# A graph-transformer kernel on one core: the usual arm's instructions in written order, with norm, linears and table pieces placed by step counters

## The chip, the core and the metric

The kernel runs on one core of a Trainium2 chip. The core has TensorE (PE: matmuls into PSUM, PEld: its weight loads), VectorE (DVE), ScalarE (ACT), GpSimd (POOL, which here issues the indirect DMAs) and SyncE (SP, which issues plain DMAs). Each engine takes its own instructions in the order of its queue. The metric is the device time of one execution in microseconds (us): 3934.97 us as the median of 10 runs of the kernel before (3932.45 to 3940.0).

## What is computed

Two layers of a heterogeneous graph transformer on 6250 nodes with 128 features (8 heads of 16), 100000 edges sorted by destination, 16 node types and 32 edge types; then a linear layer, a residual and a layer norm. Cut to what matters:

```
k, q, v = typed_linear(x, ntype, Wk), (.. Wq), (.. Wv)      # one 128x128 matrix per node type
kT, vT  = einsum(k, Watt), einsum(v, Wmsg)                  # for every node and every edge type
a       = sum_d(kT[src, etype] * q[dst]) * pri[etype] / 4   # one number per edge and head
att     = softmax of a over the edges of a destination
hag     = sum over the edges of a destination of att * vT[src, etype]
h       = silu(typed_linear(hag, ntype, Wa))
h       = h * alpha + x * (1 - alpha)                       # alpha = sigmoid(skip[ntype])
h       = (h - mean) * rsqrt(var + 1e-5) * g + b
# after two such layers: out = layernorm(x + h @ ff_w + ff_b)
```

All is float32.

## The kernel before

**Tables.** For each layer there is a table in DRAM with one row of 256 floats (kT and vT) for every pair of node and edge type: 200704 rows of 1 KB. Layer 0's is made first, together with a ranking of the nodes (the preparation, lines 239 to 674). Layer 1's table is made while layer 0's edges are worked on, from layer 0's result.

**Blocks and superblocks.** The ranking sorts nodes into 4 classes of 4 node types each, and within a class by falling degree, into 13 blocks of 128 nodes (52 in all). A block has as many *slots* as its deepest node may have edges; by `slots_of_blocks` (line 40) these are 40, 23, 21, 19, 18, 17, 17, 16, 15, 14, 13, 12, 11 in each class, 944 in a layer. One slot of a block is one indirect gather: 128 table rows, one per destination node, 128 KB. Three or four blocks make a superblock (line 188); a class has four, with 3, 3, 3 and 4 blocks and so 84, 54, 48 and 50 slots. There are 16.

**Edges** (`edges`, line 735), per block. ScalarE copies the queries of the block into PSUM (`qw`, line 744). For each chunk of up to 4 slots GpSimd issues the gathers into a `kv` tile (line 754; 12 such tiles), VectorE multiplies by the query (766) and reduces per head (768). After the last chunk VectorE adds the mask, takes the maximum and subtracts it (773 to 778), ScalarE takes Exp (780), VectorE sums the weights (782), multiplies the v half by the weight (790), adds up the chunks (795) and reduces (796). `normalized` (802) divides by the sum when the superblock is done.

**Nodes** (`nodes`, line 841), per superblock, a Python generator that yields between its steps: transpose `hag` (a TensorE matmul with the identity, line 215), mask it for each of the class's 4 types (`xm`, VectorE, line 200) and multiply by Wa (line 209), tanh (856), transpose back, mix with the old rows, statistics and norm (865 to 874), transpose. In layer 0 then the three linears for the next layer's k, v and q (`wkqv`, 209), q to DRAM, and the table pieces. In layer 1 then the final linear, residual, norm, and an indirect scatter of each block's output (922).

**Table pieces** (`table_block`, line 218), per block two pieces (16 edge types each), each in two halves (k, v). A half is 4 matmuls with 32 rows (line 229; the trace holds two records for each matmul) and 4 copies of 128x512 from PSUM to the tile `st` by ScalarE (line 236). After two halves `store` scatters the 2 MB tile into layer 1's table by an indirect DMA on GpSimd's queue (line 891). There are 104 such scatters. `st` has 3 buffers; a buffer is free again when its scatter has landed. All gathers of layer 1 wait for all of these scatters.

**Queries**: in layer 0 (`queries0`, line 719) transposes, masks, matmuls with Wq, a copy and a transpose back; in layer 1 (`queries1`, 729) a load.

**The order of the work.** `beside` (line 1006) chains the queries of the next superblock and the nodes of the one before it, pieces included; `edges` takes one step of it after each chunk and one after Exp, and runs off what is left when its blocks are done. After the last superblock its nodes run alone. This is only the order in which the program is written: the framework's scheduler, from priorities and its model of costs, then decides the order of instructions in each engine's queue, and may move them.

PSUM has 8 banks of 128x512 floats: `qwp` 2, `accp` 2 and `nps` 4, the last for all transposes, linears and table halves (the tile name `nb`).

## Time and profile before

| | us |
|---|---|
| median of 10 runs | 3934.97 |
| the profiled execution | 3931.96 |
| its span | 3930.0 |
| busy PE, DVE, ACT, POOL in the span | 1971.1, 2143.6, 921.6, 2056.4 |
| first gather of layer 0 starts | 916.4 |
| first gather of layer 1 starts | 2587.1 |
| last gather starts | 3869.4 |
| a scatter of a table piece from issue to landing, median in layer 0 | 10.8 |
| a gather from issue to landing, median | 2.8 |

A busy share here is an average over very different stages, so the span is read by its stages. A line of waits names the waiting instruction, what released it, the total, the number of times and the longest. A gap of 0.3 us between two of GpSimd's DMA issues stands there even when it waits for nothing. The granted clock of TensorE is either 0.5 or 1.0 at any moment in these records; a share in between is an average over time.

### The profile page before, as it was taken

How to read it: one execution, taken by the hardware profiler on the slowest of the kernel's cores; microseconds unless marked ns; L12 is line 12 of the kernel's file. 1: busy time of each engine (PE TensorE's matmuls, PEld its weight loads, DVE VectorE, ACT ScalarE, POOL GpSimd, SP SyncE). 2: the span in 40 equal slices, each digit the busy share in tenths (PEclk: the TensorE clock that was granted, in tenths of full speed). 3: DMA queues.
4: the chain of work that ended last, by engine and by line, in shares of the span. 5: the costliest groups of instructions: out<-in, count | busy, mean ns of one | idle time of the engine just before them, and what ended most of it. 6: DMA issues, size and time to landing. Idle time of an engine off the chain costs nothing. (4 is left out here: it accounts for less than half of the span.)

```text
span 3930.0 us, 25934 instructions
## 1 busy us (share of the span) xinstructions
PE 1971.1 (50%) x6850; PEld 1041.0 (26%) x6850; DVE 2143.6 (55%) x4929; ACT 921.6 (23%) x1928; POOL 2056.4 (52%) x2157
## 2 busy tenths in 40 slices
PE   2899957993166555666466657820221221121122
PEld 1345523331033333333234334410110110011011
DVE  6975632432655555455545554126655665665565
ACT  0244313451033232333233324420000000000000
POOL 0000072004766667656665664057776776777773
PEclk9999977995565566666666666755555555555555
DMA  4467548787366554675466558543343343333331
GB/s 89 160 273 310 235 130 328 322 342 243 105 216 218 204 205 164 245 263 207 145 239 257 200 176 305 204 159 115 110 113 95 116 113 101 110 111 106 105 103 51
DMA packets 216823, 716.14 MB, mean 182 GB/s; under 512 B 64437, under 2 KB 122670, under 8 KB 191615
## 3 DMA queue, kind: packets, MB, share of 16 engines
q0 software_dynamic: 110592, 459.50, 35.5%
q1 hardware_dynamic: 83425, 245.01, 16.3%
q10 hardware_dynamic: 22642, 9.82, 1.1%
q8 instruction: 58, 0.95, 0.1%
q14 instruction: 106, 0.87, 0.1%
HBM read 289.27 MB, written 438.40 MB: 185 GB/s over the span
## 5 line engine op out<-in xcount | busy, mean ns | idle before, releaser
L754 POOL DMA_INDIRECT kv<-tab,ell x1888 | 1794.0, 950 | 928.8 <-issue 506.2
L236 ACT COPY st<-nb 128x512 f32<-128x512 f32 x1420 | 737.8, 597 | 662.5 <-PE nb L229 425.9
L766 DVE TENSOR_TENSOR kv<-kv,qw 128x512 f32<-128x512 f32 (+3 forms) x512 | 326.1, 640 | 921.7 <-DMA kv<-tab,ell 886.2
L229 PE MATMUL nb<-bdv,kvT 32*128 32x512 f32 x832 | 388.2, 1050 | 143.0 <-ACT st L236 142.4
L229 PE MATMUL nb<-bdk,kvT 32*128 32x512 f32 x832 | 366.5, 1017 | 118.7 <-ACT st L236 118.7
L644 PE MATMUL l<-xm,wkqv 128*128 128x512 f32 (+1 forms) x832 | 394.9, 607 | 7.9 <-DVE xm L200 7.9
L215 PE MATMUL nb<-ident,hag 128*128 128x128 f32 x104 | 24.5, 366 | 596.9 <-DVE hag L809 596.9
L768 DVE TENSOR_REDUCE a<-kv 128x32 f32<-128x512 f32 (+3 forms) x512 | 319.8, 634 | 0.9
L566 POOL DMA_INDIRECT ell<-kvs,start x52 | 54.8, 1053 | 502.2 <-DVE gap L545 486.6
L200 DVE SCALAR_TENSOR_TENSOR xm<-ntb,nb 128x384 f32<-128x384 int32 (+1 forms) x256 | 133.1, 580 | 311.4 <-PE nb L215 311.4
L215 PE MATMUL nb<-ident,hs 128*128 128x128 f32 x104 | 32.6, 457 | 520.2 <-DVE hs L874 482.1
L891 POOL DMA_INDIRECT tab<-st,row x104 | 104.5, 1005 | 337.0 <-ACT st L236 322.3
L780 ACT ACTIVATE qw<-a 128x136 f32<-128x136 f32 (+11 forms) x104 | 30.7, 296 | 997.9 <-DVE a L778 980.1
L229 PEld LDWEIGHTS nb<-bdv,kvT 32*128 32x128 f32 x832 | 190.0, 285 | 263.1 <-ACT st L236 262.3
L795 DVE TENSOR_TENSOR acc<-kv,acc 128x512 f32<-128x512 f32 (+3 forms) x408 | 257.8, 632 | 0.2
L234 DVE COPY st<-nb 128x512 f32<-128x512 f32 x196 | 134.8, 688 | 212.2 <-PE nb L229 109.8
L790 DVE TENSOR_TENSOR kv<-kv,qw 128x512 f32<-128x512 f32 (+3 forms) x408 | 246.5, 623 | 0.0
L229 PEld LDWEIGHTS nb<-bdk,kvT 32*128 32x128 f32 x832 | 174.8, 276 | 213.2 <-ACT st L236 204.0
L644 PEld LDWEIGHTS l<-xm,wkqv 128*128 128x128 f32 x832 | 149.3, 195 | 237.1 <-issue 206.8
L229 PE MATMUL nb<-bdv,yT 32*128 32x512 f32 x784 | 169.3, 686 | 69.1 <-ACT st L236 66.3
L200 DVE SCALAR_TENSOR_TENSOR xm<-ntb,hT 128x512 f32<-128x512 int32 (+1 forms) x208 | 133.7, 656 | 113.6 <-PE l L644 104.0
L209 PE MATMUL nb<-xm,wkqv 128*128 128x384 f32 (+1 forms) x384 | 177.3, 630 | 20.0 <-DVE xm L200 20.0
(197 smaller groups left out, 2330.3 us busy)
## 6 DMA issues: line engine op xcount, KB each, us to landing
tab<-st SPq DMA_DIRECT2D x98, 2048.0 KB, 7.5
kv<-tab,ell POOLq DMA_INDIRECT x1888, 2.8
ntb<-typed SPq DMA_DIRECT2D x24, 192.0 KB, 3.2
xrd<-xr SPq DMA_DIRECT2D x13, 256.0 KB, 2.3
hr<-in_x_dram SPq DMA_DIRECT2D x10, 256.0 KB, 3.3
ntb<-in_node_type_dram SPq DMA_DIRECT2D x10, 256.0 KB, 6.9
hr<-xrd SPq DMA_DIRECT2D x12, 192.0 KB, 2.7
hrd<-hs SPq DMA_DIRECT2D x12, 192.0 KB, 2.4
```

Source lines behind the costliest of these rows:

```text
L200: nc.vector.scalar_tensor_tensor(xm[:, :n], ntb[:, :n], float(t), hT[:, :n], op0=ALU.is_equal, op1=ALU.mult)
L209: nc.tensor.matmul(ps[:, :n], w[:, t, :], xm[:, :n], start=(t == types[0]), stop=(t == types[-1]))
L229: nc.tensor.matmul(pt, yT[s, i * P:(i + 1) * P], bd[s, tt, :], start=True, stop=True)
L234: nc.vector.tensor_copy(to, pt)
L236: nc.scalar.copy(to, pt)
L644: nc.tensor.matmul(ps[i][:, :n], wkqv[:, i, t, :], xm[:, :n], start=(t == 0), stop=(t == TY - 1))
L754: get = nc.gpsimd.indirect_dma_start(out=kv[:, j - j0, :], out_offset=None, in_=tabs[l][:], in_offset=bass.IndirectOffsetOnAxis(ap=ell[:, ...
L766: nc.vector.tensor_tensor(kk, kk, qw[:, :D].unsqueeze(1).to_broadcast([P, j1 - j0, D]), op=ALU.mult)
L768: nc.vector.tensor_reduce(a[:, j0:j1, :], kk.rearrange("p k (h d) -> p k h d", h=H), axis=AX.X, op=ALU.add)
L790: nc.vector.tensor_tensor(to.rearrange("p k (h d) -> p k h d", h=H), v.rearrange("p k (h d) -> p k h d", h=H), w[:, j0:j1, :].unsqueeze(3) ...
L795: nc.vector.tensor_tensor(acc[:, :c], v, acc[:, :c], op=ALU.add)
L891: put = nc.gpsimd.indirect_dma_start(out=tabs[1].rearrange("(n t) c -> n (t c)", t=16), out_offset=bass.IndirectOffsetOnAxis(ap=row2[:, tg ...
```

## The change

The arm that is taken when the graph fits the slots (`arm(True)`) runs under `manual_schedule`: each engine's queue holds the instructions in the order in which the program is written. The program then places the work itself:

- `spread` gives a generator a rate in steps per slot; `tick`, called twice per chunk, advances the first entry of the list `work` and then the first of the list `pieces`. `work` holds the queries of the next superblock and the nodes of the one before. `pieces` holds the table pieces of the superblock before that. `rush` runs a generator off at once.
- The pieces leave `nodes` and become `pieces_of`. Each yield of `table_block` counts as two steps, and a scatter is issued three steps after its tile was handed over, so behind the matmuls and copies of two more halves. The output's scatters come six steps after their data, except in the last superblock. In the last superblock of layer 0, VectorE makes 2 of each 4 copies of a half.
- The second half of a block's edge work (`weighed`: sums, weights, chunks) is placed beside the next block's chunks, and the query of the next block is copied right after Exp.
- The superblocks of a class have 4, 3, 3, 3 blocks and so 103, 52, 45, 36 slots.
- PSUM: `qwp` 2, `accp` 1, `nps` 2 for transposes and linears, and 3 banks (`tps`, tile `tb`) for the table halves.
- The three linears k, v, q run one after the other over kept masks, a step each. The old rows `hr` are loaded in `nodes` (in layer 0 a second time, beside the load for the queries), `xr` one step earlier. The scaling of layer 1's edge weights moves into the first superblock's nodes.

The core of the diff:

```diff
--- before.py
+++ after.py
...
+    def scale_edge_weights():
+
         nc.vector.tensor_scalar(prit, prit, 1.0 / float(HS) ** 0.5, None, op0=ALU.mult)
         nc.vector.tensor_tensor(bdk, bdk, prit.unsqueeze(2).to_broadcast([P, RT, 2 * HS]),
                                 op=ALU.mult)
...
     load_edge_weights(0)
+    scale_edge_weights()
...
-                    pt = ps_pool.tile([P, SB * P], F32, name="nb").rearrange(
+                    pt = ps_pool.tile([P, SB * P], F32, name="tb").rearrange(
...
-        qwp = ctx2.enter_context(tc.tile_pool(name="qwp", bufs=2, space=PSUM))
-        accp = ctx2.enter_context(tc.tile_pool(name="accp", bufs=2, space=PSUM))
-        nps = ctx2.enter_context(tc.tile_pool(name="nps", bufs=4, space=PSUM))
+
+        if fast:
+            qwp = ctx2.enter_context(tc.tile_pool(name="qwp", bufs=2, space=PSUM))
+            accp = ctx2.enter_context(tc.tile_pool(name="accp", bufs=1, space=PSUM))
+        nps = ctx2.enter_context(tc.tile_pool(name="nps", bufs=2 if fast else 5, space=PSUM))
+        tps = ctx2.enter_context(tc.tile_pool(name="tps", bufs=3, space=PSUM))
...
-                    sbs.append((c * CB + i0, k, range(c * TC, (c + 1) * TC)))
+                    sbs.append((c * CB + CB - i0 - k, k, range(c * TC, (c + 1) * TC)))
+            sbs.sort(key=lambda sb: sb[0])
...
-            hr = npl.tile([P, SB, D], F32, name="hr", bufs=3)
+            hr = npl.tile([P, SB, D], F32, name="hr", bufs=2)
...
+        def q_rows(ps, k, tag):
+
+            qT = npl.tile([P, SB * P], F32, name="qT", tag="th")
...
+            q = ep.tile([P, SB, D], F32, name="q", tag=tag, bufs=2 if tag == "q" else 1)
...
-            got.append((q, types_of(i0, k), old_rows(hrd, i0, k)))
-            yield
...
-        def edges(l, i0, k, q, beside):
...
+        def edges(l):
...
+            queries = queries1 if l else queries0
+            got, work, pieces = [], [], []
+            for _ in queries(got, *sbs[0]):
+                pass
+
+            def spread(work, gen, steps, slots):
+
+                work.append([gen, steps / slots, 0.0])
+
+            def tick(n):
+                for of in (work, pieces):
+                    if of:
+                        w = of[0]
+                        w[2] += w[1] * n
+                        while w[2] >= 1.0:
+                            w[2] -= 1.0
+                            if next(w[0], of) is of:
+                                of.pop(0)
+                                break
+
+            def rush(of, gen):
+                while any(w[0] is gen for w in of):
+                    for _ in of.pop(0)[0]:
+                        pass
+
+            def slots(s):
+                return sum(KB[b] for b in range(sbs[s][0], sbs[s][0] + sbs[s][1]))
+
+            def query(s, i):
                 qw = qwp.tile([P, 512], F32, name="qw")
-                nc.scalar.copy(qw[:, :D], q[:, i, :])
...
-                    kk = kv[:, :j1 - j0, :D]
-                    nc.vector.tensor_tensor(
-                        kk, kk, qw[:, :D].unsqueeze(1).to_broadcast([P, j1 - j0, D]), op=ALU.mult)
-                    nc.vector.tensor_reduce(a[:, j0:j1, :],
-                                            kk.rearrange("p k (h d) -> p k h d", h=H),
-                                            axis=AX.X, op=ALU.add)
-                    next(beside, None)
-                av = a[:, :K, :]
-                nc.vector.tensor_tensor(
-                    av, av, neg[:, KO[b]:KO[b] + K].unsqueeze(2).to_broadcast([P, K, H]),
...
-                nc.scalar.activation(w, av, AF.Exp)
-                next(beside, None)
+                nc.scalar.copy(qw[:, :D], got[s][0][:, i, :])
+                return qw
+
+            def weighed(s, i, chunks, kvt, w, sums, den):
+
                 nc.vector.tensor_reduce(den[:, i, :], w.rearrange("p k h -> p h k"),
                                         axis=AX.X, op=ALU.add)
-
                 acc = accp.tile([P, CH, D], F32, name="acc")
                 for (j0, j1), kv in zip(chunks, kvt):
...
+                    yield
                 nc.vector.tensor_reduce(sums[:, i, :], acc.rearrange("p k c -> p c k"),
                                         axis=AX.X, op=ALU.add)
-            for _ in beside:
+                i0, k, _ = sbs[s]
+                if i == k - 1:
+                    hag = normalized(sums, den, i0, k)
+                    spread(work, nodes(l, *sbs[s], hag, got[s][1], lambda gen: table(s, gen)),
+                           16, pace(s + 1))
+
+            def pace(s):
+                s = min(s, len(sbs) - 1)
+                return slots(s) - 0.5 * KB[sbs[s][0]]
+
+            tables = {}
+
+            def table(s, gen):
+
+
+                if gen is None:
+                    if s - 2 in tables:
+                        rush(pieces, tables[s - 2])
+                else:
+                    tables[s] = gen
+                    spread(pieces, gen, 8 * sbs[s][1] + 4, (1.0 if s + 4 < len(sbs) else 0.6) * slots(min(s + 2, len(sbs) - 1)))
+
+            sums_of = None
+            qw = query(0, 0)
+            for s, (i0, k, types) in enumerate(sbs):
+                asked = None
+                if s + 1 < len(sbs):
+                    asked = queries(got, *sbs[s + 1])
+                    spread(work, asked, 6, 0.5 * KB[i0])
+                sums = ep.tile([P, SB, D], F32, name="sums")
+                den = ep.tile([P, SB, H], F32, name="den")
+                for i in range(k):
+                    b = i0 + i
+                    K = KB[b]
+                    a = ep.tile([P, max(KB), H], F32, name="a")
+                    w = qw[:, D:D + K * H].rearrange("p (k h) -> p k h", h=H)
...
+                        kk = kv[:, :j1 - j0, :D]
...
+                        tick((j1 - j0) / 2)
+                        if sums_of:
+                            next(sums_of, None)
+                        tick((j1 - j0) / 2)
+                    if sums_of:
+                        for _ in sums_of:
+                            pass
+                    av = a[:, :K, :]
...
+                    nc.scalar.activation(w, av, AF.Exp)
+                    sums_of = weighed(s, i, chunks, kvt, w, sums, den)
+
+                    if i + 1 < k:
+                        qw = query(s, i + 1)
+                    elif asked:
+                        rush(work, asked)
+                        qw = query(s + 1, 0)
+            for _ in sums_of:
                 pass
-            return normalized(sums, den, i0, k)
+            while work or pieces:
+                for of in (work, pieces, pieces, pieces):
+                    if of and next(of[0][0], of) is of:
+                        of.pop(0)
...
-        def nodes(l, i0, k, types, hag, ntb, hr):
+        def nodes(l, i0, k, types, hag, ntb, table):
             n = k * P
             last = l == L - 1
+            final = fast and i0 + k == NB
+            hr = old_rows(hrd if last else xrd, i0, k)
+            hT = transposed(nps, lambda i: hag[:, i, :], k)
+            yield
+            y = nps.tile([P, SB * P], F32, name="nb")
+            typed_linear(npl, types, ntb, hT, n, [(y, wa)])
+            yield
+
+            th = npl.tile([P, SB * P], F32, name="th")
+            nc.scalar.activation(th[:, :n], y[:, :n], AF.Tanh, scale=0.5)
 
             hb = npl.tile([P, SB, D], F32, name="hb")
             for i in range(k):
                 nc.scalar.activation(hb[:, i, :], hr[:, i, :], AF.Copy,
                                      scale=beta[:, l, i0 + i:i0 + i + 1])
-            hT = transposed(nps, lambda i: hag[:, i, :], k)
...
+            if last:
+                xr = npl.tile([P, SB, D], F32, name="xr", tag="hr", bufs=2)
+                nc.sync.dma_start(xr[:, :k], rows(xrd, i0, k))
+            else:
+                nc.sync.dma_start(rows(hrd, i0, k), hs[:, :k])
             yield
             if not last:
-                nc.sync.dma_start(rows(hrd, i0, k), hs[:, :k])
-                ps = [nps.tile([P, SB * P], F32, name="nb") for _ in range(3)]
-                typed_linear(npl, types, ntb, hT, n, [(ps[i], wkqv[:, i]) for i in range(3)])
+                if fast and i0 == 0:
+                    scale_edge_weights()
+                if fast:
+
+                    xms = list(masked(npl, types, ntb, hT, n))
+                    yield
+                    table(None)
+                outs = []
+                for j in range(3):
+                    ps = nps.tile([P, SB * P], F32, name="nb")
+                    outs.append(ps)
+                    if fast:
+                        for t, xm in xms:
+                            nc.tensor.matmul(ps[:, :n], wkqv[:, j, t, :], xm[:, :n],
+                                             start=(t == types[0]), stop=(t == types[-1]))
+                        yield
+                        if j < 2:
+                            to = npl.tile([P, SB * P], F32, name=f"kvT{j}", bufs=2)
+                            nc.scalar.copy(to[:, :n], ps[:, :n])
+                            outs[j] = to
...
+                q = yield from q_rows(outs[2], k, "qn")
                 yield
...
                 nc.sync.dma_start(rows(qrd[1], i0, k), q[:, :k])
...
-                    yield from table_block(ep, nps, kT, vT, i, (), 3 if fast else 2, store)
+                table(pieces_of(i0, k, outs[0], outs[1], (1, 3) if final else ()))
...
-            xr = npl.tile([P, SB, D], F32, name="xr", tag="hb")
-            nc.sync.dma_start(xr[:, :k], rows(xrd, i0, k))
...
-                stats(mv, i, f[:, s])
...
+            yield
+            for i in range(k):
+                stats(mv, i, f[:, i * P:(i + 1) * P])
...
-                nc.gpsimd.indirect_dma_start(
-                    out=out, out_offset=bass.IndirectOffsetOnAxis(ap=node[:, b:b + 1], axis=0),
-                    in_=o[:, i, :], in_offset=None, bounds_check=N - 1, oob_is_err=False)
+                if final:
+                    put_out(o, i0, i)
+
+            for _ in range(6):
+                yield
+            for i in range(0 if final else k):
+                put_out(o, i0, i)
+
+        def pieces_of(i0, k, kT, vT, share):
+
+
...
+            def scatter(tg, st, b):
...
+            def steps(gen):
+
+                for _ in gen:
+                    for _ in range(2):
+                        for what in late:
+                            what[0] -= 1
+                        while late and late[0][0] <= 0:
+                            scatter(*late.pop(0)[1])
+                        yield
+
+            for i in range(k):
+                def store(tg, st, b=i0 + i):
+                    late.append([3, (tg, st, b)])
+
+                yield from steps(table_block(ep, tps, kT, vT, i, share, STB, store))
+            while late:
+                yield from steps(iter((0,)))
...
-            if not fast:
+            if fast:
+                edges(l)
+            else:
                 edges_any(l)
...
-
-            def beside(s, done):
-
-                if s + 1 < len(sbs):
-                    yield from queries(got, *sbs[s + 1])
-                if done is not None:
-                    yield from nodes(l, *sbs[s - 1], *done)
-
-            done = None
-            for s, (i0, k, types) in enumerate(sbs):
-                q, *of = got[s]
-                hag = edges(l, i0, k, q, beside(s, done))
-                done = (hag, *of)
-            for _ in nodes(l, *sbs[-1], *done):
-                pass
...
     with tc.If(full < 1) as cmp:
         with ExitStack() as ctx2:
+            ctx2.enter_context(tc.manual_schedule())
             arm(True)
```

## The prediction

> **What bounds the kernel now.** The profiled execution took 3931.96 us, 3930.0 of them span; the median of the runs is 3934.97. I sum against 3930.0 and add the two differences (2.0 and 3.0) at the end. I read the page's totals and slices first, then the start times of the gathers (L754) in GpSimd's timeline to cut the span, then busy time by those stretches, then GpSimd's waits in the first of them, then single rows of the timeline.
>
> ```profile
> POOL 0000072004766667656665664057776776777773
> PEclk9999977995565566666666666755555555555555
> ```
> ```profile
> 916.00:2417.00 1501.00, 839.56 (x2212) 475.47 (x2212) 795.48 (x1843) 437.91 (x926) 981.56 (x1027) 0.61 0.60 205
> 2417.00:2587.00 170.00, 141.64 (x405) 83.49 (x404) 38.00 (x116) 92.61 (x183) 20.64 (x22) 0.68 0.61 246
> 2587.00:3870.00 1283.00, 226.12 (x552) 131.60 (x552) 782.07 (x2095) 59.47 (x180) 941.88 (x989) 0.52 0.38 108
> 3870.00:3926.00 56.00, 17.69 (x44) 10.10 (x44) 28.01 (x99) 1.43 (x3) 7.24 (x8) 0.56 0.07 17
> ```
> The second fence has busy us of PE, weight loads, DVE, ACT, POOL, then granted clock, DMA share, GB/s. The gathers start at 916.4 (layer 0), and the 945th, layer 1's first, at 2587.1. So there are five pieces: preparation 916.4 us, layer 0's stream 1501.9 (to the end of its last gather, 2418.3), a bridge of 168.8, layer 1's stream 1283.2 (to 3870.3), a tail of 59.7.
>
> ```profile
> 1130.92 0.95 POOL L754 DMA_INDIRECT kv<-tab,ell  x1 [0.30 <-issue]
> 1132.17 1.02 POOL L891 DMA_INDIRECT tab<-st,row  x1 [0.30 <-ACT st L236]
> 1133.50 0.98 POOL L754 DMA_INDIRECT kv<-tab,ell  x1 [0.30 <-issue]
> ```
> A gather holds GpSimd for 1.25 us from start to start, a scatter of a table piece for 1.33 and the gather behind it for 1.28, so 1.36 per scatter. Layer 0 gathers 944 times and scatters 84 times before the bridge: 944 x 1.25 + 84 x 1.36 = 1294. The stream took 208 more. Whose?
>
> ```profile
> POOL tab L891 <- ACT st L236: 177.5, 48, 8.4
> POOL kv L754 <- DVE acc L790: 22.9, 5, 6.3
> POOL kv L754 <- DMA tab<-st,row: 18.9, 7, 4.2
> ```
> Less 0.3 us of ordinary gap per time, these three make 201 of the 208. **GpSimd sets the end, and its loss in layer 0 is mostly a scatter standing in its queue before ScalarE has copied the piece.** Behind it wait only gathers, and VectorE waits for those. Layer 1 by the same count: 1180 + 45 output scatters x 1.35 = 1241, so 42 lost.
>
> **Layer 0's stream in the new order.** Each scatter is now issued two halves after its own last copy (a half is 4 matmuls of L229 and 4 copies of L236; a piece, two). Walking the counters of the diff through the slot counts (superblocks of a class have 103, 52, 45, 36 slots, a class 236) gives: 91 scatters before the last gather, 13 after; the pieces of superblock s run almost wholly during s+2; norm and linears of s during s+1. GpSimd's floor is 1180 + 91 x 1.36 = 1304.
>
> That takes the named wait away only if TensorE keeps pace, and the table's PSUM goes from a share in 4 buffers to 3 of its own. All queues keep source order: a matmul that waits for a buffer holds the linears behind it, whose masks and norms VectorE waits for.
>
> ```profile
> 2551.71 2.36 ACT L236 COPY st<-nb 128x512 f32<-128x512 f32 x4 [0.39 <-PE nb L229]
> 2554.46 1.77 ACT L236 COPY st<-nb 128x512 f32<-128x512 f32 x3 [0.39 <-PE nb L229]
> ```
> ```profile
> 2546.00:2580.00 34.00, 34.00 (x103) 24.21 (x98) 0.00 (x0) 27.78 (x50) 5.84 (x6) 0.50 0.85 358
> 2482.00:2494.00 12.00, 12.00 (x52) 7.18 (x50) 0.00 (x0) 11.59 (x24) 3.05 (x4) 1.00 0.88 370
> ```
> With four buffers at clock 0.50 a half takes 2.75 us: one buffer's cycle is two records of 1.06 us (832 records stand for 416 matmuls) plus a copy and its hand-over, 0.63. Estimates from these rows: three buffers back to back give 2.75 x 4/3 = 3.65 a half; a half that stands alone starts three matmuls together and the fourth after the first copy, 2.1 + 0.65 + 2.1 = 4.85. At clock 1.00 (records of 0.59) the same sums give 2.4 and 2.9. Which clock? 0.61 in the stream, with TensorE busy 56%; 0.68 in the bridge, with the same mix and TensorE busy 83%. Where TensorE is the bound the bridge is the nearer row, full clock 36% of the time: 4.15 alone, 3.2 in a row. With three quarters alone I take **3.9 us a half**: 47 us for a superblock of 3 blocks, 62 for one of 4. The linears and transposes of a superblock cost now, in the stream, wkqv 0.87 a matmul, wq 1.25, wa 0.75 at 384 columns, 12 + 4 + 4 of them, plus transposes 4.3: 23 us (28 at 512 columns); times 0.61/0.68, 21 (25).
>
> TensorE against GpSimd, per superblock of the class (us; GpSimd has slots x 1.25 + scatters x 1.36):
> - 103 slots: 68 against 137. 52 slots, with the linears of the 4-block superblock: 72 against 73. 45 slots, with its pieces: 83 against 67. 36 slots: 69 against 53.
>
> The excess is 32 a class. The lead of two halves, some 9 us, is free once a class: 23. In the last class the factor 0.6 puts 40 halves into the final 105 slots: 40 x 3.5 (more in a row) + 55 of linears = 195 against 105 x 1.25 + 19 x 1.36 = 157, so 38 over, 29 net. Sum of stalls 3 x 23 + 29 = 98, taken as **100**; the stream becomes 1404 (98 less than now). Bounds: 0 to 40 if all runs at full clock (halves 2.6, linears 0.71 a matmul in the timeline there: 12 x 2.6 + 17 = 48 against 53), 350 if TensorE stays at 0.50.
>
> Hidden otherwise: DVE has at most 49 us of work in the 53 us of the shortest superblock (10 chunks of four instructions of 0.64, 3 x 1.8 of softmax, 1 for the division, 14 for norm and masks, 3 for Exp's round trips); the DMA share of 0.60 becomes at most 0.75; kv buffers (12 chunks of 4 slots, freed a block later than now) allow a lead of 6 to 8 chunks, 2 only behind the 40-slot block (0 to 10 us a class). A tile st is needed again six steps after its scatter, in the 36-slot superblock 8 slots or 13 us with scatters, against 10.8 to land. SyncE's 16 added loads of hr in layer 0 (2.7 us to land) queue behind stores; only a query's first transposes wait for one, up to 3 us, within the bounds. Moving the scaling of the edge weights (0.42 + 1.22 us of DVE) off the start saves 0 to 6: GpSimd's 6.3 us wait at 983. Query copies ahead and Exp's wait under the next block cost about 0.9 us of DVE a block, hidden by the gathers.
>
> **Bridge.** From 2418.3 to 2587.1 the program ends 6 pieces, then does linears and pieces of two superblocks one after the other.
> ```profile
> 2417.39 0.95 POOL L754 DMA_INDIRECT kv<-tab,ell  x1 [0.31 <-issue]
> 2587.07 0.99 POOL L754 DMA_INDIRECT kv<-tab,ell  x1 [4.30 <-issue]
> ```
> New: last block's weighting 6; 12 halves of superblock 14 between the steps of 15, 47 + 16; 10 for steps left uncovered; 12 halves in a row 12 x 3.2 = 38; last landing 5: **122** (105 to 145; the split of the copies with DVE gains little, three buffers being the limit).
>
> **Layer 1.** Floor 1180 + 46 x 1.35 = 1242. The output's scatters come six steps after their data, so their waits go; of 42 I leave 13: **1255** (1245 to 1275). The tail ends with 3 blocks, not 4: **49** (45 to 60).
>
> **Sum:** 916.4 + 1404 + 122 + 1255 + 49 = 3746; with 2 and 3, **3751 us**. A change under 0.2% (8 us) can't be told from none.
>
> A page speaks against the change. In this profile the clock stayed at 0.50 for 34 us of unbroken table matmuls through four banks, and it rose only beside dense linears. The Trainium skill, "TensorE: Matmul & The Clock Gate", section "A second HAM failure mode: psum-queue depth-cycling", says that cycling through PSUM banks leaves small idle gaps in which the clock falls back and throughput suffers; three banks would then mean half clock throughout, the bound of 350. The same page, Part 1, "What's actually happening", says that one busy window of about 3.4 us releases the full clock; a crowded TensorE would then run at 1.0, the bound of 0 to 40. The 34 us row contradicts this second one for such matmuls; I keep the bridge's mixture.
>
> **Rivals.**
> - *TensorE keeps up* (its denser queue holds the full clock): stalls 25, bridge 110, tail 45, layer 1 1245: 916 + 1329 + 110 + 1245 + 45 + 5 = **3650**. For it: clock 0.96 from 100 to 300 us, where linears alternate with table halves. Against: 0.61 in the stream.
> - *TensorE becomes the bound: slower.* At half clock a half alone is 4.85 and a superblock's linears about 30; the windows are then 95, 107, 88 against 73, 67, 53, some 88 a class net: stalls 350, bridge 140, layer 1 1270, tail 55: 916 + 1654 + 140 + 1270 + 55 + 5 = **4040**. It decides once the stalls pass 100 + 184 = 284, 74% of the way from 100 to 350, that is when a half costs some 4.6 us and a superblock's linears 28. For it: TensorE in order already makes DVE wait, in VectorE's waits of the stream:
> ```profile
> DVE xm L200 <- PE nb L215: 252.0, 21, 35.4
> ```
>   Against: bursts of linears still raise the clock.
> - *The order hardly changes*, the present one already putting most steps there: **3935**. Against: the 35.4 us wait above, which steps spread this finely can't leave.
>
> **Chances:** forecast 0.55 (its own range 3680 to 3870), TensorE keeps up 0.22, slower 0.17, order unchanged 0.06. Faster 0.78, same 0.05 (most of the last case; its other 0.01 counts as faster), slower 0.17. The range takes in nearly all of the second case and the start of the third: 3630 to 3950.
>
> **What would show it.** Right: GpSimd's wait for st about 100 us, in the superblocks of 45 and 36 slots; gathers of layer 0 spanning 1360 to 1450; bridge 105 to 145. Wrong: scatter waits above 284, or granted clock in the stream above 0.75 with hardly any waits; a new wait of gathers for kv buffers; layer 1 longer than 1283.

## The result, and the profile after

The changed kernel takes **4111.8 us** (median; 4103.5 to 4121.3) where the kernel before takes 3934.97. It is slower: the ratio is 1.0448 (95% interval 1.0439 to 1.0457). The forecast was 3751, with a range of 3630 to 3950. The profiled execution took 4109.35 us, 4107.6 of them span. Ten runs below fell on chips where the kernel before itself took 4318 to 4357 us and VectorE's instructions at times started 0.5 to 7 us late behind one another, so these ten are only compared with what ran beside them on the same chip.

The page's lines for GpSimd and the granted clock:
```profile
POOL 0000170007745765576546654067666766676763
PEclk9999969975666666656665666655555555555555
```
GpSimd's digits fall to 4 and 5 again and again in layer 0's part, where before two were under 6 between its ends, and in layer 1's part most sevens have become sixes. The clock is what it was. So an engine that does the same work does it with more holes. The stretches are bounded as in the prediction, by the first and last gather of each layer; the columns are length, then busy us of PE, weight loads, DVE, ACT and POOL, then clock, DMA share and GB/s:
```profile
917.00:2551.00 1634.00, 1008.36 (x2346) 412.18 (x2346) 896.12 (x1903) 473.64 (x981) 989.85 (x1034) 0.62 0.59 197
2551.00:2684.00 133.00, 111.37 (x271) 46.52 (x271) 35.64 (x79) 50.93 (x99) 13.77 (x15) 0.62 0.56 220
2684.00:4045.00 1361.00, 216.69 (x543) 125.77 (x543) 891.23 (x2090) 53.03 (x181) 943.60 (x990) 0.53 0.36 102
```

| us | before | forecast | after | after, with the scheduler (e2) |
|---|---|---|---|---|
| preparation | 916.4 | 916.4 | 917.1 | 922.7 |
| layer 0's gather stream | 1501.9 | 1404 | 1633.9 | 1408.4 |
| of it stalls, over 1.25 per gather and 1.36 per scatter | 208 | 100 | 332 | 106 |
| bridge | 168.8 | 122 | 133.0 | 125.7 |
| layer 1's gather stream | 1283.2 | 1255 | 1360.6 | 1260.9 |
| of it stalls, with 1.35 per output scatter | 42 | 13 | 119 | 20 |
| tail | 59.7 | 49 | 62.9 | 50.1 |

The last column is the experiment that decides the case: it is the changed program with one line taken out, and its terms come out near the forecast's.

GpSimd's largest wait for another engine in layer 0's stream (waiting instruction, releaser, total us, times, longest):
```profile
POOL tab L1036 <- ACT st L239: 309.0, 60, 20.4
```
The scatters' wait for ScalarE's copy, 177.5 us before, is 309.0 now: it didn't go, it grew. 60 of the 90 scatters start within 0.5 us of the end of their own tile's last copy, although the program has two further halves written between the two. In the kernel before it was 48 of 84.

How one of these waits comes about shows in the timeline (start, length, engine, line, what, idle time before it and its releaser). TensorE:
```profile
1224.22 1.11 PE L218 MATMUL nb<-ident,hr 128*128 128x128 f32 x4 [7.91 <-DMA hr<-xrd]
...
1230.01 6.31 PE L212 MATMUL nb<-xm,wq 128*128 128x512 f32 x8
1236.25 1.13 PE L232 MATMUL tb<-bdv,kvT 32*128 32x512 f32 x6
```
A transpose of the next queries stands ahead of a table half, and waits 7.91 us for its rows. The queries' linears (6.31 us, behind VectorE's masks) stand ahead of the second half. So that half's copies end at 1239.8. GpSimd meanwhile:
```profile
1240.07 1.02 POOL L1036 DMA_INDIRECT tab<-st,row  x1 [13.07 <-ACT st L239]
1243.13 0.98 POOL L842 DMA_INDIRECT kv<-tab,ell  x1 [2.04 <-issue]
```
It stood at the scatter for 13.07 us, with the next gathers behind it. And VectorE:
```profile
1247.81 0.29 DVE L854 TENSOR_TENSOR kv<-kv,qw 128x128 f32<-128x128 f32 x1 [13.96 <-DMA kv<-tab,ell]
```
It had nothing it might do for 13.96 us, because the multiply at the head of its queue needs the late gather; the division by the sums and the masks for the next linear stand behind that multiply. A wait on one engine has become a wait on three.

### The profile page after: what moved, and what is told of

It is laid out like the page before. It is cut to its first block, busy times and chain, and to the rows that moved or that the text cites. A ratio compares the mean times of both kernels' runs of the same rounds, so it can differ in the third digit from the quotient of the medians.

```text
span 4107.6 us, 25863 instructions
## 1 busy us (share of the span) xinstructions
PE 2108.5 (51%) x6850; PEld 939.9 (23%) x6850; DVE 2353.5 (57%) x4953; ACT 911.0 (22%) x1904; POOL 2058.0 (50%) x2157
## 5 line engine op out<-in xcount | busy, mean ns | idle before, releaser
L239 ACT COPY st<-tb 128x512 f32<-128x512 f32 x1396 | 744.5, 592 | 1106.3 <-PE tb L232 1003.1
L232 PE MATMUL tb<-bdk,kvT 32*128 32x512 f32 x832 | 377.8, 896 | 105.7 <-ACT st L239 105.7
L232 PE MATMUL tb<-bdv,kvT 32*128 32x512 f32 x832 | 394.3, 937 | 55.2 <-ACT st L239 54.9
L237 DVE COPY st<-tb 128x512 f32<-128x512 f32 x220 | 151.4, 689 | 264.9 <-PE tb L232 167.8
L212 PE MATMUL nb<-xm,wa 128*128 128x384 f32 (+1 forms) x256 | 168.0, 830 | 166.5 <-DVE xm L203 166.5
L218 PEld LDWEIGHTS nb<-ident,hag 128*128 128x128 f32 x104 | 17.4, 209 | 916.7 <-issue 697.4
L988 PE MATMUL nb<-xm,wkqv 128*128 128x384 f32 (+1 forms) x384 | 197.1, 676 | 16.4 <-DVE xm L203 16.4
L232 PE MATMUL tb<-bdv,yT 32*128 32x512 f32 x784 | 171.7, 698 | 64.6 <-ACT st L239 63.0
L232 PEld LDWEIGHTS tb<-bdk,kvT 32*128 32x128 f32 x832 | 116.0, 247 | 270.2 <-ACT st L239 238.1
L232 PEld LDWEIGHTS tb<-bdv,kvT 32*128 32x128 f32 x832 | 126.0, 257 | 221.3 <-ACT st L239 192.7
```

The source lines that it names most:

```text
L212: nc.tensor.matmul(ps[:, :n], w[:, t, :], xm[:, :n], start=(t == types[0]), stop=(t == types[-1]))
L232: nc.tensor.matmul(pt, yT[s, i * P:(i + 1) * P], bd[s, tt, :], start=True, stop=True)
L237: nc.vector.tensor_copy(to, pt)
L239: nc.scalar.copy(to, pt)
L988: nc.tensor.matmul(ps[:, :n], wkqv[:, j, t, :], xm[:, :n], start=(t == types[0]), stop=(t == types[-1]))
```

## The experiments

**The order of the queues alone: e2 and e3c.** e2 is the changed kernel without its manual schedule, so that the framework's scheduler orders the queues of the new program. e3c is the kernel before with the manual schedule, with the buffers of q and qT as in the change.
```diff
# e2, in after.py
-            ctx2.enter_context(tc.manual_schedule())
# e3c, in before.py
+            ctx2.enter_context(tc.manual_schedule())
```


> The changed program in every other part, but its instructions ordered by the framework's scheduler again. Theory of order: the loss is what queues in written order do (a late load, mask or copy holds all that is written behind it); then layer 0's stream goes from 1634 back to 1480 to 1530, layer 1's gathers from 1361 to about 1285, and the time to 3890 to 3960. Theory of banks: three banks for table halves and two for the rest are the limit whoever orders; then layer 0's stream stays above 1590, only layer 1 gains, and the time is 4000 to 4050.

> The kernel before, in written order on all engines, and nothing else but a buffer of its own for the next layer's queries (without it that order can't run) and a shared one for qT. Theory of order: its scatters stand right behind their copies and all pieces of a superblock follow its linears, so layer 0's stream is longer than 1634 and the time 4150 to 4450. Rival: written order itself costs little and the new placement or the banks do; then the time is 3930 to 4000.

e2: **3768.89 us, 0.9566 of before** (0.9551 to 0.9582). Its stretches for the two streams, and its wait for the copies:
```profile
923.00:2331.00 1408.00, 1000.62 (x2343) 430.28 (x2343) 837.61 (x1906) 482.27 (x983) 989.82 (x1034) 0.64 0.69 230
...
2457.00:3718.00 1261.00, 213.86 (x554) 127.56 (x554) 790.14 (x2097) 59.60 (x179) 943.27 (x989) 0.52 0.39 110
```
```profile
POOL tab L1036 <- ACT st L239: 78.8, 32, 8.1
```
Compare the first line with that of the changed kernel: TensorE is busy 1000.6 against 1008.4 us at clock 0.64 against 0.62, GpSimd 989.8 against 989.9. The instructions are the same, and the stretch is 226 us shorter, under both ranges that were expected. 30 scatters instead of 60 start within 0.5 us of their copy; the median lead of a tile over its scatter is 6.1 us instead of 0.3.

VectorE's busy time does differ: 837.6 against 896.1 us in layer 0's stream, 790.1 against 891.2 in layer 1's. Both kernels have 4953 VectorE instructions, and their lengths add up to 2499 (e2) and 2519 us; what differs is which one follows which. A multiply and what comes behind it, in the changed kernel, then in e2:
```profile
3001.74 0.69 DVE L854 TENSOR_TENSOR kv<-kv,qw 128x512 f32<-128x512 f32 x1 [0.57 <-DMA kv<-tab,ell]
3002.47 0.69 DVE L857 TENSOR_REDUCE a<-kv 128x32 f32<-128x512 f32 x1
```
```profile
2801.58 0.69 DVE L854 TENSOR_TENSOR kv<-kv,qw 128x512 f32<-128x512 f32 x1 [2.75 <-DMA kv<-tab,ell]
2802.19 0.55 DVE L203 SCALAR_TENSOR_TENSOR xm<-ntb,nb 128x384 f32<-128x384 int32 x1
```
Written order puts the reduction right behind the multiply that it needs, and it starts 0.035 us after that ends (median). The scheduler puts a mask there that doesn't need it, and such an instruction starts 0.08 us before the end. By the tiles' names, 2262 neighbours are of the first kind in the changed kernel and 990 in e2; 1272 times 0.115 us is an estimate of 146 of the 171 us by which VectorE is busier over the whole run. How much of the time this costs was not tested by itself.

e3c: 4285.53 us, 1.0885 (1.0867 to 1.0903), with 339 us of stalls in layer 0 and 310 in layer 1. Its waits in layer 1:
```profile
POOL out_dram L922 <- DVE o L920: 255.2, 15, 18.5
```
So written order costs the new program 4111.8 - 3768.9 = 343 us and the old one 4285.5 - 3939.8 = 346 (its run of before beside it). The new placement, with the other parts of the change, gains 171 under the scheduler (3939.8 - 3768.9). The change is the sum of a gain of about 170 and a loss of about 340.

**Output scatters: e1.** The output's scatters write rows of different nodes, but each waited for the one before it to land. e1 declares them independent, as both kernels do for the table's.
```diff
+            if fast:
+                for other in outs_put:
+                    tc.declare_no_dep(put.ins, other.ins, reason="rows of other nodes")
+                outs_put.append(put)
```


> The changed kernel, with no dependence between the output's scatters (rows of different nodes). Theory on layer 1: the loss there (its gathers span 1361 us against 1283) is the output's scatters, now issued three or four in a row, each waiting some 2.0 us for the landing of the one before. Then about 36 such waits go: layer 1's gathers span some 1275 to 1290 and the time falls by 70 to 85, to about 4035. Rival: VectorE, in written order, is late, and the waits only show at the output's scatters; then they come back as waits of gathers for kv buffers and the time stays within 15 of 4112. Layer 0 is the same for both.

4052.79 us, 1.029 (1.0273 to 1.0307): 59 less than the change, where 70 to 85 were expected. Layer 1's stream is 61 shorter (1360.6 to 1300.0), layer 0's unchanged. GpSimd in the changed kernel, then in e1:
```profile
3301.83 1.02 POOL L1068 DMA_INDIRECT out_dram<-o,node  x1 [2.15 <-DVE o L1020]
3304.92 1.00 POOL L1068 DMA_INDIRECT out_dram<-o,node  x1 [2.07 <-DVE acc L795]
3307.98 0.98 POOL L1068 DMA_INDIRECT out_dram<-o,node  x1 [2.06 <-DVE kv L854]
```
```profile
3285.28 1.02 POOL L1069 DMA_INDIRECT out_dram<-o,node  x1 [2.68 <-DVE o L1021]
3286.61 1.00 POOL L1069 DMA_INDIRECT out_dram<-o,node  x1 [0.30 <-DVE kv L855]
3287.92 0.98 POOL L1069 DMA_INDIRECT out_dram<-o,node  x1 [0.30 <-DVE kv L791]
```
The waits above are about 2.07 each whatever releaser the line names: it is the landing of the scatter before. The change writes the scatters of a superblock in a row, so each pays it; where gathers stand between two of them, as the scheduler puts them, nothing is paid. The first of a group still waits for `o` in e1: 33.6 us in 10 waits over the stream. Six steps of the program were not always enough of a lead.

**The node rows' load a step earlier: e4.**
```diff
             ntb, hr = types_of(i0, k), old_rows(xrd, i0, k)
+            yield
```


> The changed kernel with the loads of a superblock's queries one step ahead of the transposes that need them. TensorE's queue stood 109 us (matmuls 60, weight loads 49) for these loads in layer 0, behind a store on SyncE's queue. Theory of order and latency: a third to a half of that was on the path of the scatters; the time falls by 30 to 60, to 4050 to 4080. Theory of banks and throughput: within 10 of 4112.

4091.69 us, 1.0387 (1.037 to 1.0404): 20 less than the change, all in layer 0. TensorE's wait for hr fell from 60.0 to 20.0 us, so half of what it no longer waited came out at the end. The result lies between the two expectations; the late load is one of the causes, and a small one.

**Four banks for the table halves: e5b, e5c.** The same kernel twice. To make room, `acc`, the sum of the weighed values, goes from PSUM to SBUF.
```diff
-            accp = ctx2.enter_context(tc.tile_pool(name="accp", bufs=1, space=PSUM))
+            accp = ctx2.enter_context(tc.tile_pool(name="accp", bufs=1))
-        tps = ctx2.enter_context(tc.tile_pool(name="tps", bufs=3, space=PSUM))
+        tps = ctx2.enter_context(tc.tile_pool(name="tps", bufs=4 if fast else 3, space=PSUM))
-            o = npl.tile([P, SB, D], F32, name="o")
+            o = npl.tile([P, SB, D], F32, name="o", tag="hb")
```


> The changed kernel, still in written order, with four PSUM banks for the table halves instead of three: the sum of the weighed values (acc) goes to SBUF to make room, and o takes hb's buffer. In the changed kernel the layer-0 gather stream takes 1633.9 us, of which 332 are stalls of the gather queue over its issue work. Theory of banks (TensorE can't run far enough ahead with three banks, so that it is the bound): the stalls fall to that of before or under it, so the stream to 1400 to 1530 and the time to 3880 to 4010. Theory of order (latencies of one engine are paid on another since nothing may pass; the banks are not full when the scatters wait): the stream stays within 50 us of 1634, the time at 4050 to 4130.

> The same kernel as the one with four banks for table halves, again for the same reason. It was ahead of the other three in that call in layer 0 (1675 against 1720 to 1763 us). Theory of banks: stalls from 332 to 100 to 230, the stream to 1400 to 1530, the time to 3880 to 4010. Theory of order: the stream stays within 60 us of 1634, the time at 4040 to 4130, since a fourth bank only lets TensorE run one more half ahead.

e5b (on a chip with before at 4318.28): 1.0249 (1.0213 to 1.0285). e5c: 4058.6 us, 1.0307 (1.029 to 1.0325). Layer 0's stream is 1572.6, 61 less than in the change and far from the 1400 to 1530 of the banks' theory; the bridge is 106 instead of 133; layer 1 is 34 longer. TensorE's table matmuls in layer 0, in the changed kernel and then in e5c (records, busy us, mean ns, idle time before):
```profile
L232 PE MATMUL tb<-bdv,kvT 32*128 32x512 f32 x720 | 338.1, 929 | 51.8 <-ACT st L239 51.8
L232 PE MATMUL tb<-bdk,kvT 32*128 32x512 f32 x728 | 324.7, 885 | 102.4 <-ACT st L239 102.4
```
```profile
L232 PE MATMUL tb<-bdv,kvT 32*128 32x512 f32 x720 | 215.9, 869 | 63.5 <-ACT st L239 63.1
L232 PE MATMUL tb<-bdk,kvT 32*128 32x512 f32 x728 | 190.0, 821 | 22.3 <-ACT st L239 21.8
```
The two lines of a kernel overlap in part: together these matmuls keep TensorE busy 589.6 us in the changed kernel and 387.5 in e5c. In the whole stream TensorE's busy time falls by 220 us (1008.4 to 788.6), and the stream by only 61. An engine that set the end would have given back more of it. The edit also has a cost: GpSimd is busy 1007.8 us in the stream instead of 989.9, because of `acc` (see e10), so by estimate the bank itself is worth up to some 80.

**Gathers ahead, node steps first, scatters later: e8, e8c, e9, e6.** e8 and e8c are one kernel: the gathers of a chunk are written up to two chunks before VectorE's work on it.
```diff
+                        here[0] += 1
+                        while len(made) < min(len(line), here[0] + 2) and (
+                                len(made) < here[0] or len(made) - 12 < spent[0]):
+                            fetch()
# e9
+                        tick((j1 - j0) / 2)
                         kk = kv[:, :j1 - j0, :D]
...
-                        tick((j1 - j0) / 2)
# e6
-                    late.append([3, (tg, st, b)])
+                    late.append([5, (tg, st, b)])
```


> The changed kernel with the gathers of a chunk written two chunks ahead of VectorE's work on it (as far as twelve kv buffers allow), all else in written order. Theory of order as a closed loop (a scatter that waits holds the gathers behind it, whose landing time VectorE then waits out in front of the node steps, so that the next scatter is late too): VectorE's waits for gathers (543 us in the layer-0 stream) fall by half or more, the stream's stalls from 332 to 100 to 220, so the stream to 1400 to 1520; the layer-1 stream also shortens by 20 to 60 from 1361 as its gathers stand ahead of the output scatters; the time is 3800 to 3980. Theory of banks or TensorE: the scatters wait as before, the stream stays at 1590 to 1640 and the time at 4020 to 4110.

> The changed kernel with the first half of a chunk's steps written ahead of VectorE's multiply and reduction of that chunk instead of behind them, all queues in written order. Only VectorE's order changes against the other engines: its node steps no longer stand behind the wait for that chunk's gathers. Theory of the closed loop: the node steps come up to one gather latency earlier and the stalls of the layer-0 stream fall from 332 to 180 to 290, the time to 3960 to 4070. Theory of banks or TensorE: no change beyond 20 us in the stream.

> The changed kernel with the scatter of a table half written five steps behind its data instead of three. Theory of order: a scatter stands too early in GpSimd's queue; two more steps (about 8 to 11 us of gathers) let ScalarE's copy be done when the queue comes to it, so the waits for st of 309 us fall to 120 to 220 and the stream to 1450 to 1570, the time to 3930 to 4050. Theory that the table pieces' throughput is the bound (TensorE and its banks): the wait moves to another place and the stream stays within 30 us of 1634, since the same halves must still be made.

> The same kernel as the one with gathers written two chunks ahead, run again because the earlier call fell on a chip on which the kernel before took 4318 us instead of 3935. On a chip like the first one, theory of the closed loop through the gathers: VectorE's waits for gathers in the layer-0 stream fall from 543 to under 300 us, the stalls of the gather queue from 332 to 150 to 230, the time to 3880 to 4000. If the loop does not run through the gathers (the scatters wait because ScalarE and VectorE come to the table halves late for their own order): the gather waits fall, but the stalls stay at 290 to 340 and the time at 4020 to 4115.

e8, e9 and e6 ran beside e5b (before at 4318.28): e8 1.0318 (1.0284 to 1.0351), e9 1.0428 (1.0395 to 1.0461), e6 1.0518 (1.0485 to 1.0551). The changed kernel wasn't run beside them, so e9 and e6 can't be set against it; against e8 they are 53 and 88 us longer. Ratios don't carry over from one kind of chip to the other: the kernel of e8 and e8c is 1.0318 on one and 1.0128 on the other. e8c: **3985.41 us, 1.0128** (1.0111 to 1.0144), 126 less than the change. Layer 0's stream is 1523.0 with 225 us of stalls instead of 332, layer 1's 1318.1 instead of 1360.6; the bridge is 25 longer. VectorE's waits in layer 0 in the changed kernel, then those of e8c with GpSimd's:
```profile
DVE kv L854 <- DMA kv<-tab,ell: 543.2, 133, 21.1
DVE kv L854 <- ACT qw L778: 101.2, 40, 19.4
```
```profile
DVE kv L868 <- ACT qw L778: 305.5, 46, 29.5
...
POOL tab L1050 <- ACT st L239: 196.8, 45, 17.8
DVE kv L868 <- DMA kv<-tab,ell: 184.4, 77, 8.9
```
The gathers' landing was part of the loop: VectorE's wait for it falls by 359 us. Much of that comes back as a wait for ScalarE's query copy (101 to 306), which stands in ScalarE's queue behind copies of table halves: in those 306 us ScalarE copies halves for 135 and stands for 98 at such a copy until TensorE has made its half. The scatters' wait falls by 112. This edit also puts each scatter behind two more chunks of gathers, which e6 alone does in another way, so how much of the 107 is VectorE's earlier start and how much the later scatter isn't separated.

**All repairs in written order: e13, and without the fourth bank: e15, e17, e19; with another buffer for o: e16.**


> The changed kernel in written order with every repair at once: gathers two chunks ahead, four banks, the node rows' load a step earlier, output scatters free of each other. If the written order costs what these four places show, layer 0 comes to 1430 to 1530 and layer 1 to 1260 to 1300, the time to 3780 to 3920, under the kernel before. If it is the order as a whole (each engine's next instruction often not the one that could run), more than half of the scheduler's gain stays out of reach: layer 0 at 1530 to 1620, the time at 3920 to 4040.

> The changed kernel in written order with the three repairs of order alone: gathers two chunks ahead, the node rows' load a step earlier, output scatters free of each other; three banks as in the change. If the gains add up: layer-0 stalls 332 - 107 - 20 = 205, so the stream 1490 to 1520, layer 1 1361 - 43 - 60 = 1258 to 1285, the time 3870 to 3930, at or under the kernel before. If the banks decide once the gathers are ahead, the stream stays at 1515 to 1550 and the time at 3930 to 3970. If order was nearly all of it, the stream comes under 1450 and the time under 3850.

> The kernel in written order with all four repairs (3818 us; layer 1 1293 us) and o in kvT0's buffer. If the shared buffer cost it: layer 1 1255 to 1275 and the time 3785 to 3805. If acc in SBUF: unchanged within 8 us.

e13: **3818.18 us, 0.9705** (0.9689 to 0.9722), with 121 us of stalls in layer 0 and 51 in layer 1.
```profile
POOL tab L1052 <- ACT st L239: 81.0, 33, 12.2
```
That is e2's wait (78.8) without a scheduler. In layer 0, where the single repairs gave 107 (gathers), 61 (bank) and 20 (load), together 188, all of them give 332 - 121 = 211. So the loss has places: the four repairs give back 294 us (4111.8 - 3818.2), where the scheduler gives 343. The fourth bank is no matter of order, though, and helps the scheduler too: against e10 below, which has the bank, written order with all repairs is still 73 us longer. e15, e17 and e19 are one kernel, run on chips with before at 4331, 4353 and 4357 us: 1.0214, 1.0185 and 1.0194 (intervals within 0.004 of each). e16, beside e15, is 0.9951 (0.9929 to 0.9973), 70 us shorter in layer 0's stream: there only the kernel with the fourth bank comes, just, under the kernel before. On the first kind of chip the three order repairs alone haven't run. If the gains of e8c, e1 and e4 added up, they would take 3985 - 59 - 20 = 3906, an estimate.

**The scheduler with the repairs: e10, and with another buffer for o: e14, e18.**


> The new program without the manual schedule (3769 us, 0.957 of before) with the three small repairs: output scatters free of each other, the node rows' load a step earlier, four banks for table halves. Layer 0 has 106 us of stalls left and layer 1 has 20. Theory of order: the scheduler has already filled those waits, so the gain is small: 3730 to 3775. Theory of banks: the remaining 79 us of waits for halves go, 3670 to 3730.

> The version with the scheduler, four banks, the earlier load and free output scatters (3745 us; layer 1 1286 us), with o in the buffer of kvT0, which is idle in layer 1, instead of hb's. If sharing hb's buffer cost the 25 us against the scheduler alone (1261): layer 1 1250 to 1265, the time 3715 to 3730. If acc in SBUF costs it: layer 1 stays at 1280 to 1295 and the time at 3740 to 3755.

e10: **3745.05 us, 0.9511** (0.9495 to 0.9527), the fastest kernel of the study, under the kernel before and the changed one. Layer 0 has 67 us of stalls, the bridge is 99; layer 1 is 1286, 25 longer than with the scheduler alone. e14 and e18 (one kernel; before at 4331 and 4353) are 0.9701 (0.967 to 0.9733) and 0.966 (0.9629 to 0.9691). They were to tell whether `o` in hb's buffer costs those 25 us or `acc` in SBUF, and ran on the other kind of chip, where their times don't tell. GpSimd's busy time does. Layer 1's stream in e10, to set beside e2's (943.27):
```profile
2390.00:3676.00 1286.00, 204.25 (x529) 122.12 (x529) 782.59 (x2040) 55.17 (x172) 967.34 (x990) 0.53 0.38 107
```
24 of the 25 us are in GpSimd's own issues. Layer 1's 944 gathers hold it 911 to 927 us in all seven runs with `acc` in SBUF, whichever buffer `o` has and on either kind of chip, and 895 to 899 us in every other kernel; the fourth bank has no work in layer 1. Of e10's 87 gathers there that take over 1.1 us (the median is 0.95), 82 run while VectorE adds into `acc`. In e2, with `acc` in PSUM, 316 gathers run beside such an addition and none takes that long. So it is `acc`. Why e10's tail is 68 us against 50 stays open.

## Why the prediction was wrong

The sign was wrong, by one step. Of 361 us between forecast and time, 230 are in layer 0's stream, 106 in layer 1's, 11 in the bridge, 14 in the tail.

**The step that failed: "That takes the named wait away only if TensorE keeps pace."** The stall was worked out as the excess of TensorE's work over GpSimd's in each superblock. That prices the written order as a load on one engine. The sentence before the clock question, that a matmul that waits holds the linears behind it and VectorE waits for these, named the coupling, and no term of the sum held it. Three superblocks of the changed kernel in a row, with 52, 45 and 36 slots:
```profile
1443.00:1533.00 90.00, 61.57 (x147) 24.28 (x147) 57.39 (x125) 28.99 (x60) 55.62 (x59) 0.67 0.57 197
1533.00:1619.00 86.00, 69.56 (x161) 27.33 (x159) 45.61 (x105) 32.33 (x67) 50.14 (x53) 0.63 0.60 208
1619.00:1698.00 79.00, 57.49 (x132) 21.93 (x130) 42.18 (x100) 26.10 (x55) 39.67 (x42) 0.61 0.64 222
```
I had 72, 83 and 69 us of TensorE's work against 73, 67 and 53 of GpSimd's. TensorE was busy 62, 70 and 57, or 67, 77 and 62 with its waits for copies of halves, which my price of a half includes. That is less than I priced, and the windows last 90, 86 and 79. No engine is full in any of them. Of the 332 us of stalls, some 100 fall into superblocks of 103 and 52 slots, where the sum had next to none. What the runs show in place of the load is the wait for ScalarE's copies, 309 us, that goes round the queues: 79 under the scheduler, 81 in written order with the four repairs.

**The lead "of two halves, some 9 us"** was counted in steps of the program. In time it was 0.3 us at the median: the reading is that as soon as one engine waits, the others run up to the same place in the program, and a lead that is written becomes a lead of nothing.

**The bounds of 0 and 350** came out of the clock and the banks. The stalls, 332, are inside, and past the 284 from which the slower rival was to decide. But that rival's mechanism, TensorE at half clock as the bound, did not happen: the clock was 0.62, and e2 does TensorE's same work, through the same three banks, in 226 us less. That its 4040 is near the time is luck. Two of the prediction's own signs of being wrong did appear: scatter waits above 284, and layer 1 longer than 1283. The section "A second HAM failure mode: psum-queue depth-cycling" in the Trainium skill's "TensorE: Matmul & The Clock Gate" would have the clock suffer from cycling through banks; here it was 0.62 in this stretch with three banks and 0.64 with four (e5c), against 0.61 before, so the loss is not one of clock.

**Layer 1: "the output's scatters come six steps after their data, so their waits go."** They did not go: 119 us of stalls against 13. The step counted the wait for the data and not the wait of each scatter for the one before it, 61 us by e1; nor the first one's wait for `o`, some 30. The profile before showed the output scatters' waits in its total of 42 us, and I did not ask what they would wait for once written in a row.

**What was right.** The floor of GpSimd (90 scatters, 91 forecast), the preparation, and the bridge within its bounds (133, 105 to 145). The placement was worth what the sum says, under the scheduler: 1408 against 1404, 126 against 122, 1261 against 1255, 50 against 49, 3769 against 3751. What was not priced is the line that takes the scheduler away. The match is in part luck, because the places don't match. Of e2's 106 us of stalls, 41 fall into the 103-slot superblocks, where the sum had none, and 14 into the four 45-slot ones, where it had 16 each. And a half took 4.4 us in e2 and 4.1 in the changed kernel (TensorE's busy time for these matmuls plus its waits for the copies, over 181 halves), where 3.9 was priced.

**Left open:** how e8c's gain splits between VectorE's earlier start and the scatter's later place; what e6 and e9 do on a chip like the first; the order repairs alone on such a chip; what VectorE's dependent neighbours cost by themselves; and what makes up the last 73 us between e13 and e10.

## What to carry to other kernels

When a change takes the order away from a scheduler, price that by itself, before the placement: run the new program both ways, or list for every queue what stands behind each instruction that can wait, and follow the ring to the engine where it began. A sum of busy times per window says how short a window can get, not how long written order makes it; a lead must be counted in microseconds at the engine that waits, and it lasts only while nobody waits. Where the order is written by hand, issue loads and gathers well ahead of the work on them, put other work between dependent scatters and between dependent VectorE instructions, and give the engine in the middle a spare buffer.

## What was not expected of the hardware

- **The fourth PSUM bank makes the table matmuls cheaper, not only earlier.** The same 1448 records of 32-row matmuls keep TensorE busy 590 us through three banks and 388 through four, while a single record's mean falls by only 60 to 64 ns. On average 2.2 records run at once through three banks and 3.2 through four (their lengths added up, over the busy time). In the timeline above, three matmuls of a half take 1.13 us together, and the fourth starts 1.8 us after they began, behind a copy. In e5c all four (eight records) go in 1.14 us:
```profile
1565.69 1.14 PE L232 MATMUL tb<-bdk,kvT 32*128 32x512 f32 x8
```
  The section "Why this matters for your kernels" of the Trainium skill's "TensorE: Matmul & The Clock Gate" says that matmuls with few rows run at once if they sit in distinct row groups; the trace agrees: the four start within 0.02 us.
- **Dependent scatters in a row cost 3.06 to 3.09 us each**, start to start, against 1.31 to 1.33 for independent ones; the difference is the landing of a 64 KB write, and neither the releaser's name in the line nor the queue's busy time shows it.
- **Where VectorE's sum lies sets how long GpSimd's DMA issues take.** With `acc` in SBUF, gathers that are issued during the additions into it take 1.03 us on average and up to 1.53 in e10's layer 1; with `acc` in PSUM (e2) 0.95 and at most 1.05.
- **On VectorE a dependent neighbour costs some 0.115 us more than an independent one**, 0.035 us after the end against 0.08 us before it, and written order made 2262 of them where the scheduler left 990.
